# A row-modulated MLP and routed low-rank layer on one core: the last block's sixth and seventh outer products on two levels, its first rows leaving by accumulating stores

## The chip, the cores and the metric

The kernel runs on one core of a Trainium2 chip. The metric is device time in microseconds (us), the median of the runs shown. All arithmetic is in float32.

## The reference, cut to what matters

```python
# cond: x (64, 64, 512), q (64, 256)
q_emb = relu(q @ W3 + b3)
v = (n * x + sum(x, axis=1, keepdims=True)) * q_emb[:, None, :]
y = relu(v @ W2 + b2)                       # first 512x512 product
# ffn
base = y @ W_base + b_base                  # second 512x512 product
shared = (y @ A_s) @ B_s                    # rank 16
gates = softmax(y @ W_router + b_router)    # 6 experts
w = gates where among the two largest, else 0
routed = sum_e w_e * (y @ A_r[e]) @ B_r[e]  # rank 16 each
out = x + base + shared + routed
```

There are 4096 rows of 512 features.

## The kernel before, in words

The rows lie transposed, features on the 128 partitions. They are worked in four blocks (`k` = 0 to 3) of 1024 rows; a block has two halves `h` of 512 rows and two pairs `f` of 128-feature chunks.

Each 512x512 product is done by a Strassen scheme (the form with seven products and shared sums): over the two row halves and two feature halves, seven outer products, numbered 1 to 7, replace eight. `row_sums` makes the sums of rows (`sy`), `weight_sums` those of weights (`tb`, `t2`). An outer product can itself be done by the same scheme, in seven 128x256 products instead of eight: this is "two levels". `inner_row_steps` makes its four row sums, `inner_weight_side` its four weight sums.

An outer product on two levels is called by its place `t` in a list `order`. Its inner products are the calls `q(n, t)`, n = 1 to 7, into two PSUM banks, `a` and `b`, each split in a low half `lo` and a high half `hi`: 1 and 2 go to a-lo, 5 and 3 to a-hi, 6 to b-lo, 7 and 4 to b-hi. The chain between them is:

- `seed_y(t)`: ScalarE copies a-lo to b-lo; q(6, t) adds on top of it.
- `seed_z(t)`: ScalarE copies b-lo to b-hi; q(7, t) adds on top, and `take_22(t)` reads b-hi out before q(4, t) adds again.
- `take_w5(t)`, `take_u(t)`, `take_22(t)`, `take_11(t)`, `take_12(t)` and `take_21(t)` bring the results out to SBUF. They are copies on ScalarE where nothing is added (`plus` is None), and additions on VectorE else; `take_1` is `take_11` and `take_12`.

In the second product of block 3 (`second_inner`), `order` is (1, 2, 5, 4, 3): these five are on two levels. Outer products 6 and 7 are plain: `product(bank["y", j], 6, ...)` and `product(bank["z", j], 7, ...)`, four 128x512 matmuls each, seeded by `seed` on ScalarE. Their results are added to `x12`, `x21` and `x22`, the tiles of the residual rows, by VectorE. `x11` takes p1 (on GpSimd), the second outer product and the routed part (`pr`, on VectorE), and leaves by `leave` on SyncE's queue.

The instructions of each engine run in the order in which the Python code issues them; waits are on semaphores. `gate` makes the softmax and the ranks from `ph` on VectorE, with other work placed in it by `between`; `weigh` makes `hw`, `turn` transposes it to `hwT` (TensorE, then two ScalarE copies), `routed` adds the low-rank part to a bank. `difference` makes `hwd` on GpSimd. GpSimd also makes most inner row sums and issues the accumulating stores (`accum_op=ALU.add`) of blocks 1 and 2, whose rows had been written from `x1` to the output in DRAM beforehand, in `load_rows`.

`first_inner` is the first product of blocks 1 to 3, on two levels throughout; `relus` writes y; POOL's L603 and L606 make `e3` and the last `p5`. `wide_sums` lays out the weight sums of the second product's inner levels.

Of the kernel before, what the change touches and what calls it, by code (L numbers as in the profile page):

```python
# [16 lines left out]
P = 128  # L17
# [21 lines left out]
def adaln_ffn(ctx: ExitStack, tc: tile.TileContext, xa, x0, x1, head, w3, w2, wb, a, bcat, bb, br, outT):  # L39
# [117 lines left out]
    def inner_weights(w, t, groups):  # L157

        low = w.rearrange("p (o k) m -> p o k m", k=KH)
        place, steps = {}, []  # L160
        for it, outer, engine in groups:
            if outer == (1, 2):
                b = lambda c, m: low[:, :, c, ts(m, P)]
            elif outer == (3,):
                b = lambda c, m: t[3][:, c, ts(m, P)].unsqueeze(1)
            else:
                step = 3 // (len(outer) - 1)
                b = lambda c, m, step=step: t["sums"][:, ::step, c, ts(m, P)]
            place.update((o, (it, n)) for n, o in enumerate(outer))
            steps.append(inner_weight_side(it, b, engine))  # L170

        def side(o, n):
            b = {1: t[o][:, 0, :P], 2: t[o][:, 1, :P], 3: t[o][:, 1, P:]}
            it, i = place[o]
            return b[n] if n in b else it[:, {5: 0, 6: 1, 7: 2, 4: 3}[n], i]

        return side, steps
# [302 lines left out]
    def first_inner(k, y):  # L480
# [98 lines left out]
        for step in inner[k]["late"]:  # L579
            step()  # L580
        fill(2)
        for t in range(2, 7):
            open_banks(t)
            take_1(t - 2)
            q(1, t)
            q(5, t)
            seed_y(t)
            q(4, t - 2)
            take_21(t - 2)
            q(7, t - 1)  # L590
            take_22(t - 1)
            if t > 2:
                take_u(t - 1)
            take_w5(t)
            fill(1)
            q(3, t - 1)
            q(6, t)
            seed_z(t)
            if t > 2:
                q(2, t - 1)  # L600
            if order[t - 2] == 6:
                for cols in (hi, lo):
                    nc.gpsimd.tensor_tensor(e3[:, :, cols], u[:, :, cols], p5[:, :, cols], ALU.add)  # L603
            if order[t - 2] == 7:
                for cols in (lo, hi):
                    nc.gpsimd.tensor_tensor(p5[:, :, cols], v7[:, :, cols], p5[:, :, cols], ALU.add)  # L606
            if order[t - 2] == 2:
                relus(p1, 0, 0)
            fill((1, 1, 2, 2, 0)[t - 2])
# [8 lines left out]
        relus(p5, KH, 1)  # L618
# [27 lines left out]
    def turn(k):  # L646
        pt = ps_h.tile([P, 2 * NS, P], F32, tag="ph", name=f"pt_{k}")
        hwT = small.tile([P, 2, TB], F32, tag="hwT", name=f"hwT_{k}")
        for s in range(2 * NS):
            nc.tensor.transpose(pt[:GB, s, :], hw[:, s, :], ident)  # L650
        for h in range(2):
            nc.scalar.copy(hwT[:GB, h], pt[:GB, ts(h, NS)].rearrange("p s t -> p (s t)"))  # L652
        return hwT
# [6 lines left out]
    def gate(k, ph, between=()):  # L660
# [30 lines left out]
        nc.vector.tensor_tensor(eq, gj, ge, ALU.is_equal)  # L691
        others()
        nc.vector.tensor_tensor(gt, gj, ge, ALU.is_gt)
        nc.vector.tensor_tensor(eq, eq, tri.unsqueeze(1).to_broadcast(pair), ALU.mult)
        nc.vector.tensor_tensor(gt, gt, eq, ALU.add)
# [5 lines left out]
    def load_rows(k):  # L701

        res = {}
        for n, (f, h) in zip(pair_tags[2:3] + pair_tags[:2] + pair_tags[3:], ((1, 0), (1, 1), (0, 0), (0, 1))):
            if (f, h) == (0, 0) and 0 < k < NB - 1:

                nc.sync.dma_start(outT[k, :KH, h], x1[k, :KH, :, ts(h, TB)])
                continue
# [6 lines left out]
    def second_between(k, y, res):  # L715
# [72 lines left out]
        def main_part(ph):  # L788
# [40 lines left out]
            hwT = turn(k)  # L829
# [45 lines left out]
    def second(k, y, ph, res):  # L875
# [65 lines left out]
        hwT = turn(k)  # L941
# [134 lines left out]
    def second_inner(k, y, res):  # L1076


        order = (1, 2, 5, 4, 3)
        lo, hi = slice(0, R2), slice(R2, TB)  # L1080
        plain = xpool.tile([P, NC, 2, TB], F32, tag="x", name="inner_y").rearrange("p c h t -> p (c h t)")
        plain = plain.rearrange("p (n o t) -> p n o t", n=4, o=4)
        parts = mid.tile([P, 4, KH, TB], F32, tag="s", name=f"parts_{k}")
        p1, p5 = (parts[:, n] for n in range(2))
        x11, x12, x21, x22 = res[0, 0], res[1, 0], res[0, 1], res[1, 1]
# [4 lines left out]
        s_side, sums_of = row_places(lambda o: sy[o], {o: (plain[:, :, i], at) for o, (i, at) in places.items()})  # L1090
        plus = {1: None, 2: x11, 5: None, 4: x21, 3: x12}
        out = {1: p1, 2: x11, 5: p5, 4: x21, 3: x12}

        def passed_on(t, j, cols):
            o = order[t]
            if o == 5:
                add(x12[:, j, cols], x12[:, j, cols], p5[:, j, cols])
                add(x22[:, j, cols], x22[:, j, cols], p5[:, j, cols], nc.gpsimd)
# [19 lines left out]
        of_y = lambda f, h: lambda c, r: y[:, f + c, h, ts(r, R2)]  # L1118
        run(sums_of(1, of_y(0, 0), nc.gpsimd))

        def row_side():
# [5 lines left out]
            fourth.extend(steps[3:])  # L1127

        def late_sums():
            of_s = lambda o: lambda c, r: sy[o][:, c, ts(r, R2)]  # L1130
            run(sums_of(5, of_s(5), nc.gpsimd))
            run(sums_of(4, of_y(KH, 1), nc.gpsimd))
            run(fourth)
            run(sums_of(3, of_s(3), nc.gpsimd))
# [3 lines left out]

        def first_part():
            open_banks(0)  # L1140
            q(1, 0)
            q(5, 0)
            seed_y(0)
            take_w5(0)
# [6 lines left out]
        def leave(f, h, t):  # L1151
            for j in range(KH):
                nc.sync.dma_start(outT[k, f + j, h], t[:, j])

        def seed(j, name, source):
            bank[name, j] = ps_p.tile([P, TB], F32, tag="pp", name=f"o{name}_{k}_{j}")
            nc.scalar.copy(bank[name, j], source)

        def main_part(ph):
            open_banks(1)  # L1160
            q(1, 1)
            q(5, 1)
            seed_y(1)
# [11 lines left out]
            gate(k, ph, (first, lambda: tools.take_12(0)))  # L1175
            q(4, 0)
            take_21(0)
            q(7, 1)
            take_22(1)
            take_u(1)  # L1180
            q(3, 1)
            q(2, 1)
            weigh(k, ph)
            late_sums()
            take_1(1)
            for j in range(KH):
                seed(j, "y", p1[:, j])
                product(bank["y", j], 6, j, tb, sy, start=False)
            q(4, 1)
            take_21(1)  # L1190
            for j in range(KH):
                seed(j, "z", bank["y", j])
                add(x12[:, j], bank["y", j], x12[:, j])
            product(bank["z", 0], 7, 0, tb, sy, start=False)
            hwT = turn(k)
            hws["second"] = hwT[:GB, 1]
            product(bank["z", 1], 7, 1, tb, sy, start=False)
            for j in range(KH):
                for x in (x21, x22):
                    add(x[:, j], bank["z", j], x[:, j])  # L1200
            add(x11, x11, p1, nc.gpsimd)
            hws["less"] = difference(k, hwT)[:GB]

            for t in (2, 3):
                open_banks(t)
                q(1, t)
                q(5, t)
                seed_y(t)
                take_w5(t)
            pr = ps_h.tile([P, 2 * NS, P], F32, tag="ph", name=f"pr_{k}")  # L1210
            pr = pr.rearrange("p (j s) t -> p j (s t)", j=KH)
            for j in range(KH):
                accumulate(pr[:, j], bcat_sb[:, ts(j, P)], hwT[:GB, 0], True)
            add(x11, pr, x11)
            leave(0, 0, x11)
            q(2, 2)
            q(6, 2)
            take_u(2)
            seed_z(2)
            q(3, 2)  # L1220
            routed(2, 1)
            q(6, 3)
            take_u(3)
            seed_z(3)
            q(7, 2)
            routed(2, 22)
            take_22(2)
            q(2, 3)
            take_1(2)
            open_banks(4)  # L1230
            q(1, 4)
            q(5, 4)
            seed_y(4)
            q(4, 2)
            routed(2, 4)
            take_21(2)
            q(7, 3)
            routed(3, 22)
            take_22(3)
            take_w5(4)  # L1240
            q(3, 3)
            q(6, 4)
# [4 lines left out]
                    for n, (b, at) in enumerate(((bank["b", 4], slice(R2, R2 + P)), (other, slice(0, P))))]  # L1247
            for n, b, cols in last:
                nc.scalar.copy(b, bank["b", 4][:, ts(n, P)])
            routed(3, 1)  # L1250
            take_1(3)
            q(4, 3)
            routed(3, 4)
            take_21(3)
# [5 lines left out]
            take_u(4)  # L1260
            q(3, 4)
            q(2, 4)
            routed(4, 1)
            take_1(4)
# [26 lines left out]
    def wide_sums():  # L1291
        place = xpool.tile([P, NC, 2, TB], F32, tag="x", name="inner_tb").rearrange("p c h t -> p (c h t)")
        wide["parts"] = place[:, 12 * P : 12 * P + 2 * KH * TB].rearrange("p (n j t) -> p n j t", n=2, j=KH)
        place = place[:, : 12 * P].rearrange("p (n o m) -> p n o m", n=4, o=3)
        high, wide["steps"] = inner_weights(
            wb_sb, tb, [(place[:, :, :2], (5, 4), nc.gpsimd), (place[:, :, 2:], (3,), nc.gpsimd)]
# [3 lines left out]
    for k in range(NB):  # L1300
        y = mid.tile([P, NC, 2, TB], F32, tag="y", name=f"y_{k}")
# [4 lines left out]
        else:  # L1306
# [4 lines left out]
            if k == 1:  # L1311
                for step in wide["steps"][1]:
                    step()
# [87 lines left out]
```

## Time and profile before

| | us |
|---|---|
| median of 3 runs | 253.21 (253.17 to 253.36) |
| span of the profiled execution, first to last instruction | 251.6 |
| TensorE busy | 246.9 |
| VectorE busy | 203.0 |
| ScalarE busy | 158.1 |
| GpSimd busy | 126.1 |
| granted TensorE clock | 1.000 |

No time of the profiled execution other than its span is recorded; the span lies 1.6 us below the median.

In the profile PE is TensorE, PEld its weight loads, DVE VectorE, ACT ScalarE, POOL GpSimd, SP SyncE. A row of a timeline gives start, duration, engine, line of the kernel, operation, what is written from what, shapes, and in brackets the idle time ahead of it and what ended it. TensorE does one float32 matmul in two passes, and each is a record: "x2" is one 128x256 product, "x4" two of them or one pair. Block 3 begins at about 189.7 us, its second product at about 216 us.

### The profile page before, as it was taken

The page shows a single profiled execution, that of the slowest core. Times are in us where ns is not written, and L with a number is a line of the kernel's source. Part 1 is how long each engine was busy: PE and PEld are TensorE (multiplying, and loading weights), DVE is VectorE, ACT ScalarE, POOL GpSimd, SP SyncE. Part 2 cuts the span into 40 slices and gives each one's busy share as a digit, 9 for nine tenths or more (in the row PEclk, how much of TensorE's full clock was granted, in tenths as well). Part 3 has the DMA queues.
Part 4 walks back from the last instruction along what each step waited for, and adds up shares of the span by engine and source line. Part 5 has one row for each costly group of instructions (what it writes and reads, how often), then busy time and mean ns, then how long its engine had stood idle before and what let it go on. Part 6 is the DMA issues. An engine that isn't in the chain of part 4 may idle for free.

```text
span 251.6 us, 3678 instructions
## 1 busy us (share of the span) xinstructions
PE 246.9 (98%) x1134; PEld 189.5 (75%) x1134; DVE 203.0 (81%) x407; ACT 158.1 (63%) x436; POOL 126.1 (50%) x150
## 2 busy tenths in 40 slices
PE   8999999999999999999999999999999999999993
PEld 4745897454468889857888889957888889966783
DVE  2899998879996888999994788999992577797472
ACT  2299588579017889797638889796836428252320
POOL 1000000009707589059479978339649984059850
PEclk9999999999999999999999999999999999999999
DMA  6998818000431024835559923306269953400054
GB/s 182 364 343 288 330 32 304 0 3 9 157 125 42 3 86 180 319 123 217 68 82 198 154 85 104 124 26 249 20 81 194 157 134 92 164 1 0 6 195 136
DMA packets 17482, 33.82 MB, mean 134 GB/s; under 512 B 1605, under 2 KB 3781, under 8 KB 17462
## 3 DMA queue, kind: packets, MB, share of 16 engines
q1 hardware_dynamic: 13910, 27.09, 30.6%
q0 software_dynamic: 3264, 6.29, 15.9%
q10 hardware_dynamic: 288, 0.20, 0.3%
q8 instruction: 9, 0.15, 0.2%
q14 instruction: 11, 0.09, 0.1%
HBM read 19.94 MB, written 14.68 MB: 138 GB/s over the span
## 4 chain that ended last, share of the span: by engine, by line
PE 98%; DVE 0%; issue 0%
PE ia L502 14%; PE ph L1338 11%; PE ib L502 11%; PE ha L988 10%; PE hb L988 8%; PE oz L181 7%; PE py L409 6%; PE oy L181 6%; PE ja L988 4%; PE jb L988 3%; PE ox L181 3%; PE ow L181 3%; PE idle L192 2%; PE yw L181 1%; PE pt L650 1%; PE yx L416 1%
## 5 line engine op out<-in xcount | busy, mean ns | idle before, releaser
L229 ACT ACTIVATE x<-x,vsum,nq 128x64 f32<-128x64 f32 x176 | 63.2, 432 | 1.0 <-DVE vsum L221 1.0
L657 POOL TENSOR_TENSOR hwd<-hwT 113x512 f32<-113x512 f32 x4 | 5.1, 1272 | 55.4 <-ACT hwT L652 55.4
L1338 PEld LDWEIGHTS ph<-a_sb,y 128*128 128x128 f32 x256 | 30.6, 192 | 0.7
L1338 PE MATMUL ph<-a_sb,y 128*128 128x118 f32 x256 | 30.6, 274 | 0.0
L493 DVE TENSOR_TENSOR u<-ib,u 128x256 f32<-128x256 f32 x42 | 16.4, 418 | 13.0 <-PE ib L502 12.9
L493 DVE TENSOR_TENSOR u<-ia,u 128x256 f32<-128x256 f32 (+1 forms) x36 | 16.0, 461 | 6.2 <-ACT u L540 4.7
L508 ACT COPY ib<-ia 128x256 f32<-128x256 f32 x21 | 7.6, 361 | 18.0 <-PE ia L502 18.0
L395 ACT ACTIVATE y<-u,head_sb 128x256 f32<-128x256 f32 (+1 forms) x30 | 15.8, 584 | 3.6 <-DVE u L468 3.0
L502 PE MATMUL ib<-inner_s,inner_t 128*128 128x256 f32 x60 | 17.4, 379 | 0.0
L219 DVE TENSOR_REDUCE vsum<-x 128x8 f32<-128x512 f32 x24 | 15.4, 674 | 0.0
L181 PE MATMUL oz<-sy,tb 128*128 128x512 f32 x32 | 15.0, 592 | 0.0
L181 PE MATMUL oy<-sy,tb 128*128 128x512 f32 x32 | 14.7, 598 | 0.0
L409 PE MATMUL py<-v,w_sb 128*128 128x512 f32 (+1 forms) x40 | 14.7, 518 | 0.0
L511 ACT COPY ib<-ib 128x256 f32<-128x256 f32 x21 | 7.6, 360 | 8.9 <-PE ib L502 8.5
L502 PEld LDWEIGHTS ib<-inner_s,inner_t 128*128 128x128 f32 x60 | 11.4, 190 | 1.6
L344 POOL TENSOR_TENSOR sy<-sy 128x256 f32<-128x256 f32 x4 | 3.8, 952 | 17.2 <-PE oy L181 17.2
L409 PEld LDWEIGHTS py<-v,w_sb 128*128 128x128 f32 x40 | 7.6, 196 | 6.2 <-issue 4.5
L267 ACT ACTIVATE v<-x,vsum,nq 128x64 f32<-128x64 f32 x32 | 11.1, 430 | 1.9 <-DVE vsum L265 1.9
L181 PEld LDWEIGHTS oy<-sy,tb 128*128 128x128 f32 x32 | 5.8, 190 | 6.8 <-issue 6.2
L745 POOL DMA_DIRECT2D out_dram<-y x8 | 10.7, 1723 | 0.0
L502 PE MATMUL ia<-s,t 128*128 128x256 f32 x36 | 10.2, 379 | 0.0
L181 PEld LDWEIGHTS oz<-sy,tb 128*128 128x128 f32 x32 | 5.8, 190 | 5.8 <-issue 5.3
(321 smaller groups left out, 679.4 us busy)
## 6 DMA issues: line engine op xcount, KB each, us to landing
xu<-in_x_dram SPq DMA_DIRECT2D x14, 512.0 KB, 4.6
out_dram<-xu SPq DMA_DIRECT2D x25, 256.0 KB, 2.1
x<-in_x_dram SPq DMA_DIRECT2D x12, 512.0 KB, 7.6
out_dram<-y POOLq DMA_DIRECT2D x8, 512.0 KB, 8.5
out_dram<-inner_tb POOLq DMA_DIRECT2D x4, 512.0 KB, 6.0
x<-in_x_dram SPq DMA_DIRECT2D x7, 256.0 KB, 5.9
w_sb<-in_w_dram SPq DMA_DIRECT2D x4, 256.0 KB, 5.7
wb_sb<-in_wb_dram SPq DMA_DIRECT2D x4, 256.0 KB, 5.1
```

What stands on the lines that cost most here:

```text
L181: nc.tensor.matmul(ps, w[i][:, c, ts(j, P)], s[i][:, c, :], start=start and c == 0, stop=c == KH - 1, skip_group_check=True,)
L219: nc.vector.tensor_reduce(vsum[:, c, bs], xc, AX.XY, ALU.add)
L229: nc.scalar.activation(x, x, AF.Identity, bias=bias, scale=scale)
L267: nc.scalar.activation(v[:, c, :, ts(b, NH)], batches_of(c, b, b + 1)[:, :, 0], AF.Identity, bias=vsum[:, c, b : b + 1], scale=nq[:, c, b ...
L395: nc.scalar.activation(y[:, f, h, cols], src, AF.Relu, bias=b2_sb[:, f : f + 1])
L409: nc.tensor.matmul(p[:, :, lo * NH : hi * NH], w2_sb[:, c, ts(f, P)], v[:, c, :, lo * NH : hi * NH], start=(c == 0 and lo == 0), stop=(c = ...
L493: add = lambda o, a, b: nc.vector.tensor_tensor(o, a, b, ALU.add)
L502: nc.tensor.matmul(bank[b, t][:, cols], t_side(o, n), s_side(o, n), start=n == 1, stop=True, skip_group_check=True,)
L508: nc.scalar.copy(bank["b", t][:, lo], bank["a", t][:, lo])
L745: nc.gpsimd.dma_start(outT[k, f : f + KH, h].rearrange("f p t -> p f t"), parts[o], accum_op=ALU.add)
L988: nc.tensor.matmul(p, w, s, start=start, stop=True, skip_group_check=True)
L1338: nc.tensor.matmul(ph[:, h * NS + s, :HC], y[:, c, h, ts(s, P)], a_sb[:, c, :], start=(c == 0), stop=(c == NC - 1),)
```

## The change

It touches seven things.

1. `order` becomes (1, 2, 6, 7, 5, 4, 3): the outer products 6 and 7 of block 3 are on two levels, at t = 2 and 3; products 5, 4 and 3 move to t = 4, 5 and 6. The steps of all seven are interleaved anew. Product 6 gives `u` = p1 + it, product 7 gives `z` = u + it, both kept in SBUF and added to x12, x21 and x22 as whole 128x1024 tiles.
2. Their row sums are eight new GpSimd operations beside the gate, their weight sums four 128x128 GpSimd operations in block 1 (sixth) and four in block 3 (seventh). The row sums of product 4 move ahead of those of product 1.
3. `x11` is gone. Block 3's first rows are copied from DRAM to DRAM, as in blocks 1 and 2, and p1, p2 and the routed part `r11` are added by three accumulating stores from GpSimd's queue. `r11` is copied out of PSUM by ScalarE.
4. The DRAM-to-DRAM copies are written with the 128 partitions as their first dimension.
5. The gate's ranks are made in three operations in place of four, in all four blocks.
6. In block 3 `hwd` is made by VectorE, from `hwT` and from `pt` in PSUM; the relus of p5 move ahead, between seed_y(6) and q(4, 4) of the first product.
7. `y` of block 3 is placed in a buffer of x, and its inner sums in that of y.

```diff
-            elif outer == (3,):
-                b = lambda c, m: t[3][:, c, ts(m, P)].unsqueeze(1)
+            elif len(outer) == 1:
+                b = lambda c, m, o=outer[0]: t[o][:, c, ts(m, P)].unsqueeze(1)
...
-        for step in inner[k]["late"]:
+        for step in inner[k]["late"] + (wide["steps"][2] if k == 1 else []):
             step()
...
             seed_y(t)
+            if t == 6 and k == NB - 1:
+                relus(p5, KH, 1)
             q(4, t - 2)
...
-        nc.vector.tensor_tensor(eq, gj, ge, ALU.is_equal)
+        nc.vector.tensor_tensor(gt, gj, ge, ALU.subtract)
         others()
-        nc.vector.tensor_tensor(gt, gj, ge, ALU.is_gt)
-        nc.vector.tensor_tensor(eq, eq, tri.unsqueeze(1).to_broadcast(pair), ALU.mult)
-        nc.vector.tensor_tensor(gt, gt, eq, ALU.add)
+        nc.vector.scalar_tensor_tensor(eq, gt, 0.0, tri.unsqueeze(1).to_broadcast(pair), ALU.is_equal, ALU.mult)
+        nc.vector.scalar_tensor_tensor(gt, gt, 0.0, eq, ALU.is_gt, ALU.add)
         others()
...
-        order = (1, 2, 5, 4, 3)
+        order = (1, 2, 6, 7, 5, 4, 3)
...
-        plus = {1: None, 2: x11, 5: None, 4: x21, 3: x12}
-        out = {1: p1, 2: x11, 5: p5, 4: x21, 3: x12}
+        plus = {1: None, 2: None, 6: p1, 7: u, 5: None, 4: x21, 3: x12}
+        out = {1: p1, 2: p2, 6: u, 7: z, 5: p5, 4: x21, 3: x12}
...
+        run(sums_of(4, of_y(KH, 1), nc.gpsimd))
         run(sums_of(1, of_y(0, 0), nc.gpsimd))
+
+        def to_rows(t, f=0, h=0):
+            nc.gpsimd.dma_start(
+                outT[k, f : f + KH, h].rearrange("f p t -> p f t"), t, accum_op=ALU.add
+            )
...
+            for o in (6, 7):
+                run(sums_of(o, of_s(o), nc.gpsimd))
 
         def late_sums():
+            to_rows(p1)
             run(sums_of(5, of_s(5), nc.gpsimd))
-            run(sums_of(4, of_y(KH, 1), nc.gpsimd))
             run(fourth)
+            to_rows(p2)
             run(sums_of(3, of_s(3), nc.gpsimd))
```

The new order of block 3's second product, from the gate on (what it replaces is told above):

```python
def second():
    tools.take_12(0); q(4, 0); take_21(0)
    start(2)                      # q(1, 2), q(5, 2), seed_y(2)
    q(7, 1); take_u(1); q(3, 1); take_22(1)

def third():
    q(2, 1); take_1(1); q(6, 2); seed_z(2); q(2, 2); take_w5(2)
    q(4, 1); take_21(1); q(7, 2); take_u(2); start(3)

gate(k, ph, (first, second, third))
weigh(k, ph)
late_sums()
q(3, 2); q(6, 3); seed_z(3); q(2, 3); start(4); q(7, 3)
take_22(2); take_w5(3); q(4, 2); take_1(2); take_21(2); take_w5(4)
q(3, 3); take_u(3); take_22(3)
hwT, pt = turn(k)
q(6, 4); take_u(4); seed_z(4); q(4, 3); take_1(3); take_21(3)
nc.vector.tensor_tensor(hwd[:GB], hwT[:GB, 0], of_h(1), ALU.subtract)
start(5); add(x21, x21, z); take_w5(5); q(2, 4); q(3, 4); routed(4, 1)
...                               # pr: two 113x512 matmuls
add(x22, x22, z)
r11 = ...                         # two ScalarE copies of pr
to_rows(r11)
take_1(4); q(6, 5); take_u(5); seed_z(5); q(7, 4); routed(4, 22); take_22(4)
q(2, 5); add(x12, x12, u); start(6)
q(4, 4); routed(4, 4); take_21(4); q(7, 5); routed(5, 22); take_22(5)
add(x12, x12, p5); take_w5(6); q(3, 5); q(6, 6)
...                               # the tail, as before
```

## The prediction

> **What bounds the kernel now.** I read the page's busy table and its chain first, then TensorE's timeline in the last block, then the other engines' timelines in the same stretch.
>
> ```profile
> PE 246.9 (98%) x1134; PEld 189.5 (75%) x1134; DVE 203.0 (81%) x407; ACT 158.1 (63%) x436; POOL 126.1 (50%) x150
> ...
> PE 98%; DVE 0%; issue 0%
> ```
>
> TensorE (PE) is busy for 246.9 of 251.6 us and the chain that ended last is PE alone: what shortens PE's own list shortens the kernel, and every new wait of PE lengthens it one for one. PE's timeline around the work that goes:
>
> ```profile
> 222.93 0.59 PE L988 MATMUL ja<-y,wb_sb 128*128 128x256 f32 x2
> 223.36 3.65 PE L181 MATMUL oy<-sy,tb 128*128 128x512 f32 x8
> 226.85 0.59 PE L988 MATMUL jb<-y,low_t 128*128 128x256 f32 x2
> 227.28 1.88 PE L181 MATMUL oz<-sy,tb 128*128 128x512 f32 x4
> 229.00 1.04 PE L650 MATMUL pt<-ident,hw 128*113 128x128 f32 x8
> 229.88 1.88 PE L181 MATMUL oz<-sy,tb 128*128 128x512 f32 x4
> 231.59 0.59 PE L988 MATMUL ja<-sy,tb 128*128 128x256 f32 x2
> ```
>
> Columns: start, duration, what. Durations overlap; the distance between starts is the price. No bracket of idle time stands in any row: PE has no gap here. I call one q(n,t), a 128x256 product, a step; ten of them fill 219.04 to 223.36, 0.432 us each.
>
> **TensorE's list.** The plain sixth and seventh products go: 3.49 (223.36 to 226.85), 1.72 and 1.71 us, 6.92 in all. Fourteen steps come: 14 x 0.432 = 6.05. Net -0.87. The two products for hwT (pr) and the tail stay. Without new waits: 253.21 - 0.87 = 252.34. The profiled span is 251.6, 1.6 below the median of the runs; I take those 1.6 us as unchanged, and put the difference on the median.
>
> **What a late copy costs PE.** Each two-level product needs the y-bank copied (seed_y) between its q(5,t) and q(6,t), and q(7,t)'s result taken before q(4,t) adds on top of it. The price of such a wait:
>
> ```profile
> 216.40 0.59 PE L988 MATMUL ja<-inner_y,low_t 128*128 128x256 f32 x2
> ...
> 217.03 0.36 ACT L996 COPY jb<-ja 128x256 f32<-128x256 f32 x1 [2.79 <-PE ja L988]
> ...
> 222.67 1.11 ACT L1157 COPY oy<-parts 128x512 f32<-128x512 f32 x2
> ...
> 223.31 0.30 PEld L181 LDWEIGHTS oy<-sy,tb 128*128 128x128 f32 x2 [0.19 <-ACT oy L1157]
> ```
>
> The seed starts 0.63 us after q(5,0) and ends 0.99 after it. The oy copy (0.57 as a single one) ended near 223.25, 0.11 before PE's start at 223.36; the weight load came 0.05 later, and the 8 passes took 3.49 where 8 x 0.432 is 3.46. So a result that ends 0.11 ahead of its step costs about 0.03: the wait is (end minus planned start) + 0.14.
>
> *First new wait.* In the new order the seventh product (t = 3) goes q(1,3), q(5,3), q(3,2), q(6,3): q(6,3) is two steps, 0.86 us, behind q(5,3), but the seed ends 0.99 behind it. In the kernel before the tightest pair has three steps (219.48 to 220.77). Wait: 0.99 - 0.86 + 0.14 = 0.27. Not less than 0.13 (the bare difference), and a wait cannot gain; not over 0.35.
>
> *Second new wait.* q(4,4) must wait for take_22(4) on VectorE (DVE). DVE runs take_12(4), take_u(5), take_22(4) in this order, and take_12(4) waits for ScalarE's (ACT's) take_11(4), which the new code queues behind the two 128x512 copies of pr into r11. Counted from pr's first start: ACT can start at 1.92 (a pr pair lasts 1.88 in the timeline, plus 0.04), the two copies advance ACT by about 0.5 each (the hwT pair took 1.08), take_11 ends near 3.28, the three DVE operations (0.42 each, 0.34 apart) at 3.31, 3.65 and 3.99, the last ending at 4.41. PE reaches q(4,4) after pr (1.72) and six steps (2.59): 4.31. Wait: 4.41 - 4.31 + 0.14 = 0.24; take 0.25, bounds 0.10 and 0.35. In the kernel before DVE itself added pr to x11, and ACT's copies were not behind it.
>
> **VectorE in the gate.** The three rank operations replace four: L691, L693, L694 and L695 are 0.46, 0.45, 0.45 and 0.46 (0.87 in block 3). A scalar_tensor_tensor of 128x256 is 0.42 (L255), so 288 elements are about 0.46: DVE saves one operation per block. PE is full in the gates of blocks 0 to 2, so that is worth nothing there. In block 3 the last DVE link matters: take_22(2) stands behind the gate and hw, and q(4,2) waits for it. Worked forward from unchanged rows: q(7,1) at 222.93, its bank read by ACT 223.56 to 223.93, take_22(1) to 224.37, two rank operations to 225.26, three takes of which the last waits for q(7,2) (225.52 + 0.63 = 226.15) and ends 226.57, rank 0.45, w 0.21, hw 1.08 to 228.37, take_22(2) to 228.70. It is due 0.14 before q(4,2): 229.41 + 0.27 - 0.14 = 229.54. Cover: 0.84.
>
> What can eat the cover is GpSimd (POOL). It was idle here for 10.36 us; now the eight row sums of the sixth and seventh products (0.73 each) run beside the gate, and the four of product 5 after them.
>
> ```profile
> 222.96 0.45 DVE L694 TENSOR_TENSOR eq<-eq,tri 128x288 f32<-128x288 f32 x1
> 223.44 0.87 DVE L695 TENSOR_TENSOR gt<-gt,eq 128x288 f32<-128x288 f32 x1
> ...
> 224.83 0.21 DVE L699 SCALAR_TENSOR_TENSOR w<-rank,g 128x48 f32<-128x48 f32 x1
> ...
> 223.18 0.81 POOL L344 TENSOR_TENSOR inner_y<-sy 128x256 f32<-128x256 f32 x1 [10.36 <-PE ja L988]
> ```
>
> L695 lost 0.41 when a POOL sum had just started; L699 lost nothing with POOL still at work. Three such operations (two rank ones and w) follow take_22(1). At 0.2 each, the mean of these two rows, they lose 0.6, of which 0.31 is DVE's wait for q(7,2) anyway: covered. At a full POOL sum each, 2.2 - 0.31 = 1.9, less the cover: 1.05 us of stall. I take 0.05. The operations ahead of take_22(1) have 1.3 us of waiting to lose. The Trainium skill (SBUF — State Buffer, "Who interferes with whom") says that a DVE instruction with both inputs in SBUF and a GpSimd instruction that reads SBUF exclude each other for a whole instruction, whoever comes second waiting fully; it speaks against this change, since by it all three could wait out a full sum, which is the 1.05, while the two rows give 0.05.
>
> **Covered elsewhere.** POOL's four 128x128 weight operations (0.46) in block 1 fit the 2.08 us it idled ahead of L603; if not, e3 is late one for one. The four in block 3 end near 208.7. The relus of p5, moved ahead of seed_z(6), start when L606 ends (206.99), take 1.33, and seed_z(6) ends at 208.67; q(7,6) at 208.88 needs it by 208.74: 0.07 of cover, beyond it one for one. SP has one load less into SBUF and a copy from DRAM to DRAM instead, due only when p1 leaves at 223 or later. DVE loses six adds of 0.64 and the 1.23 pr add, gains twelve takes of 0.42, the 1.22 adds and hwd (0.69, due before pr, done near 233.5 against 234.8): off the path but for the links above. Placing y in x's buffers and inner_y in y's waits for the previous block's stores, issued at 197.84 at the latest, first needed near 208.7.
>
> *The accumulating stores.* POOL is in order, and each store waits for the one before to land:
>
> ```profile
> 179.25 1.19 POOL L745 DMA_DIRECT2D out_dram<-inner_tb  x1
> 185.84 1.20 POOL L745 DMA_DIRECT2D out_dram<-inner_tb  x1 [5.39 <-DVE inner_s L344]
> ```
>
> One alone: 6.6 us from issue to the next. Behind p1 (223 to 225) are queued the sums of 5, the fourth row sum and p2 (by 232), behind p2 the sums of 3 (first needed at 238.7), behind r11 (by 238.6) the x22 adds, 3.5 us, and on SP every x22, x21 and x12 store. r11 lands near 245, the last stores go at about 247.5: covered, with 3 us.
>
> **Sum.** -0.87 + 0.27 + 0.25 + 0.05 = -0.30: 252.91, own range 252.6 to 253.2.
>
> **Rivals.** *PE absorbs the two waits* (252.34 to 252.7): the wait rule rests on one row, and a step of copy may be shorter than the rows I used. For it: no gap anywhere in the last block before. Against it: two steps are 0.86 and the copy needs 0.99. It gives over 0.51 us if both waits together stay under 0.35. *GpSimd's sums hold up the gate* (slower): at take_22(2), price up to 1.05, giving 252.91 + 1.00 = 253.91; slower than before once DVE is over 1.2 us late on that link, slower by 0.51 from 1.7 on. L695 speaks for it, L699 against. *The stores' chain ends last* (slower): if both landings take the longest the trace has (11.6, three in flight together), p2 goes at 235, r11 at 247, the x22 adds end at 251 and the span is about 4 us longer, 257; decided near 9 us a landing. Against it: nothing else is on the DMA engines there (DMA share 0.00 from 219 to 232). That the fourteen steps bring no saving is excluded by the rows.
>
> **Chances.** Forecast 0.42, absorbed 0.36, gate 0.13, stores 0.06, other waits 0.03. 0.2%, 0.51 us, is about what a measurement of this kernel can tell from no change. Faster 0.36, within 0.42, slower 0.22. Range 252.35 (no wait at all) to 253.8 (nearly all of the gate's bound).
>
> **What would show it.** Right: PE busy about 0.87 less; a weight load of q(6,3) (jb) released by ACT's seed and one of q(4,4) released by DVE, 0.2 to 0.3 us of lost PE start each. Wrong: even steps of 0.432 at both places (absorbed); a gap at q(4,2) with rank operations of 0.8 or more (gate); POOL's r11 store after 242 and SP's stores bunched behind it (chain).

## The result, and the profile after

| | before | after |
|---|---|---|
| median, us | 253.19 (6 runs, 253.01 to 253.53) | 254.62 (6 runs, 254.22 to 255.19) |
| ratio, 95% interval | | 1.006 [1.0046, 1.0074] |
| span of the profiled execution | 251.6 | 252.8 |
| from the start of TensorE's 201st matmul record to that of its last | 200.34 | 201.98 |
| from there to the end of SyncE's last instruction, 0.05 ahead of the span's end | 4.00 | 4.09 |
| granted TensorE clock | 1.000 | 0.997 |

The change is slower by 1.43 us; 252.91 was forecast, with a range to 253.8. The fourth row is the one to compare: up to the 201st matmul record the same work takes a few tenths more or less in each execution (47.19 us before, 46.72 after). From there on the kernel lost 1.63 us (taken before the two figures are rounded).

Busy line and chain of the page after:

```profile
PE 246.9 (98%) x1146; PEld 191.3 (76%) x1146; DVE 208.3 (82%) x407; ACT 159.7 (63%) x442; POOL 135.3 (53%) x167
...
PE 89%; POOL 4%; DVE 4%; issue 1%; ACT 1%; POOLq 0%; ACTq 0%
```

PE's busy time is no smaller although its list is shorter: of the waits below only 1.15 us, the two brackets in the rows that follow, show as idle time; the rest counts as busy. The chain is no longer PE alone; VectorE and GpSimd have come into it. TensorE's waits show as distances between starts above 0.432 for a step. Its timeline after, in two stretches of the last block:

```profile
226.21 0.59 PE L993 MATMUL ja<-outer_y,seventh_tb 128*128 128x256 f32 x2
227.50 0.70 PE L993 MATMUL ja<-outer_y,tb 128*128 128x256 f32 x2 [0.69 <-DVE parts L986]
228.03 0.59 PE L993 MATMUL jb<-outer_y,seventh_tb 128*128 128x256 f32 x2
...
242.84 1.03 PE L993 MATMUL ja<-hwT,bcat_sb 113*128 113x256 f32 x4
244.32 0.70 PE L993 MATMUL jb<-y,inner_tb 128*128 128x256 f32 x2 [0.46 <-DVE xu L986]
```

q(3, 2) starts 1.29 us behind q(5, 3), not 0.43, and the step after it 0.53 behind it: 0.96 lost. q(4, 5) starts 1.48 behind a row of two steps (0.86): 0.62, with the next step 0.72. Summed over all places of the trace, from the starts of the records:

| wait of TensorE | us |
|---|---|
| q(7, 6) of the first product, behind ScalarE's seed_z(6) | 0.27 |
| q(3, 2), behind VectorE's take_w5(2) | 0.96 |
| q(4, 2), q(3, 3), behind hw and take_22(2) | 0.32 |
| q(4, 4), behind VectorE's take_22(4) | 0.23 |
| q(4, 5), behind VectorE's take_22(5) | 0.72 |

Together 2.50; less the 0.87 of the list that is +1.63, which is the 1.63 found. What held VectorE at the two large ones, from the timelines of VectorE and of GpSimd:

```profile
224.13 0.74 DVE L696 SCALAR_TENSOR_TENSOR eq<-gt,tri 128x288 f32<-128x288 f32 x1
224.91 1.87 DVE L697 SCALAR_TENSOR_TENSOR gt<-gt,eq 128x288 f32<-128x288 f32 x1
226.70 0.41 DVE L986 TENSOR_TENSOR outer_y<-ja,outer_y 128x256 f32<-128x256 f32 x1
...
240.00 3.93 DVE L986 TENSOR_TENSOR xu<-xu,parts 128x1024 f32<-128x1024 f32 x1
```

```profile
223.84 0.72 POOL L347 TENSOR_TENSOR outer_y<-sy,outer_y 128x256 f32<-128x256 f32 x1
224.50 1.19 POOL L1132 DMA_DIRECT2D out_dram<-parts  x1
225.28 1.17 POOL L344 TENSOR_TENSOR inner_y<-sy 128x256 f32<-128x256 f32 x1
226.53 0.83 POOL L345 TENSOR_TENSOR inner_y<-inner_y,sy 128x256 f32<-128x256 f32 x1
...
239.77 3.07 POOL L986 TENSOR_TENSOR xu<-xu,parts 128x512 f32<-128x512 f32 x3
```

The last rank operation (L697) took 1.87 us instead of the 0.46 of its kind: it ended 0.33 after GpSimd's sum L344 (226.45). take_w5(2) stands behind it on VectorE. The addition x12 += u took 3.93 instead of 1.22: it ended 1.09 after the third of GpSimd's additions to x22 (242.84). take_22(5) stands behind that. In both, the time from the end of that GpSimd operation to VectorE's own end is what VectorE's operation takes alone less 0.13 (0.46 and 1.22 alone), as if its work began about when GpSimd was through. The take at 226.70, with one of its two inputs in PSUM, took its usual 0.41 beside GpSimd's sum L345.

### The profile page after: what moved, and what is told of

Its sections match the earlier page's. It is cut to its first block, busy times and chain, and to the rows that moved or that the text cites. A ratio compares the mean times of both kernels' runs of the same rounds, so it can differ in the third digit from the quotient of the medians.

```text
span 252.8 us, 3725 instructions
## 1 busy us (share of the span) xinstructions
PE 246.9 (98%) x1146; PEld 191.3 (76%) x1146; DVE 208.3 (82%) x407; ACT 159.7 (63%) x442; POOL 135.3 (53%) x167
## 4 chain that ended last, share of the span: by engine, by line
PE 89%; POOL 4%; DVE 4%; issue 1%; ACT 1%; POOLq 0%; ACTq 0%
PE ia L502 12%; PE ph L1372 11%; PE ha L993 10%; PE ib L502 9%; PE hb L993 8%; PE py L409 6%; PE oz L181 5%; PE oy L181 4%; PE ja L993 4%; PE ox L181 3%; PE ow L181 3%; PE jb L993 2%; DVE xu L986 2%; PE idle L192 1%; PE yw L181 1%; PE pt L653 1%
## 5 line engine op out<-in xcount | busy, mean ns | idle before, releaser
L660 POOL TENSOR_TENSOR hwd<-hwT 113x512 f32<-113x512 f32 x3 | 3.8, 1266 | 54.9 <-ACT hwT L655 54.9
L344 POOL TENSOR_TENSOR sy<-sy 128x256 f32<-128x256 f32 x4 | 3.8, 946 | 18.3 <-PE oy L181 18.3
L181 PE MATMUL oz<-sy,tb 128*128 128x512 f32 x24 | 11.3, 592 | 0.0
L181 PE MATMUL oy<-sy,tb 128*128 128x512 f32 x24 | 11.1, 597 | 0.0
L750 POOL DMA_DIRECT2D out_dram<-inner_tb x4 | 4.9, 1232 | 10.1 <-ACT y L1009 10.1
L245 DVE TENSOR_REDUCE vsum<-x 128x8 f32<-128x512 f32 (+1 forms) x10 | 5.7, 574 | 4.4 <-DMA x<-in_xa_dram 3.5
```

The lines of the kernel that those rows point to most:

```text
L181: nc.tensor.matmul(ps, w[i][:, c, ts(j, P)], s[i][:, c, :], start=start and c == 0, stop=c == KH - 1, skip_group_check=True,)
L750: nc.gpsimd.dma_start(outT[k, f : f + KH, h].rearrange("f p t -> p f t"), parts[o], accum_op=ALU.add)
```

## The experiments

All start from the kernel after, unless said otherwise. "Before" is the kernel before on the same chip in the same comparison. Waits are read as above.

| run | median | ratio to before, 95% interval |
|---|---|---|
| e1 | 253.85 | 1.0044 [1.0027, 1.0061] |
| e2 | 255.93 | 1.0128 [1.0108, 1.0147] |
| e3 | 254.43 | 1.007 [1.0041, 1.01] |
| e4 | 254.23 | 1.0048 [1.0036, 1.006] |
| e5 | 255.49 | 1.0096 [1.0081, 1.0111] |
| e6 | 253.42 | 1.002 [1.0003, 1.0038] |
| e7 | 255.58 | 1.0109 [1.0082, 1.0136] |
| e8 | 252.86 | 0.9986 [0.9971, 1.0] |
| e9 | 254.12 | 1.0051 [1.003, 1.0073] |
| e10 | 253.69 | 1.0029 [1.0019, 1.004] |
| e11 | 253.84 | 1.0047 [1.0022, 1.0071] |
| e12 | 252.95 | 0.9999 [0.9983, 1.0015] |
| e13 | 259.34 (one run) | |
| e14 | 253.82 | 1.0006 [0.9985, 1.0027] |
| e15 | 252.53 | 0.998 [0.997, 0.9989] |

### e1: the addition x12 += u earlier

```diff
             add(x22, x22, z)
+            add(x12, x12, u)
...
             q(2, 5)
-            add(x12, x12, u)
```

> One addition on VectorE moves: x12 += u (128x1024) goes from its place ahead of take_22(5) to the one behind x22 += z, where GpSimd is idle and VectorE itself idled 1.83 us. Theory (VectorE's additions from SBUF are held while GpSimd adds from SBUF): it takes 1.2 instead of 3.93 us, take_22(5) starts about 1.5 us earlier, the wait of TensorE at q(4, 5) (0.73) goes: 254.6 - 0.7 = 253.9. Rival (q(4, 5) stands behind something else, such as the stores' traffic or ScalarE's copies): 254.6.

253.85. The wait at q(4, 5) is gone, the other waits in the last block are as before the edit (0.90 at q(3, 2), 0.32, 0.23). The two additions, x22 += z and x12 += u, now take 1.18 us each:

```profile
235.39 2.36 DVE L986 TENSOR_TENSOR xu<-xu,parts 128x1024 f32<-128x1024 f32 x2
```

The term is shown: 0.7 us in the trace, by where this one addition stood (in the medians, 0.81 above before instead of 1.43).

### e2 and e3: GpSimd's stores in another order

```diff
# e2
-            to_rows(p1)
             run(sums_of(5, of_s(5), nc.gpsimd))
             run(fourth)
+            to_rows(p1)
             to_rows(p2)
```

> GpSimd's accumulating store of p1 moves behind the four row sums of product 5 and the fourth row sum, so the sums of 7 and of 5 follow one another without a store between. Theory A (each GpSimd sum from SBUF holds VectorE's two-input operations, the store adds nothing): the second rank operation stays held, 0.9 to 1.9 us, and the time stays 254.6 within 0.3. Theory B (issuing the store holds VectorE, too): the second rank operation falls to 0.9 or less, the wait at q(3, 2) from 0.96 to 0.3 or less, and the time to 253.9 to 254.0. Both theories leave the wait at q(4, 5) as it is.

```diff
# e3
-            to_rows(p1)
+            to_rows(p2)
             run(sums_of(5, of_s(5), nc.gpsimd))
             run(fourth)
-            to_rows(p2)
+            to_rows(p1)
```

> The stores of p1 and p2 change places. p2 is complete later, so GpSimd waits from the end of product 7's sums (224.6) to about 226, and VectorE's second rank operation (224.9) finds it idle; no work is left out. Theory (GpSimd's work beside it holds the rank operation, sum or store): 0.46 instead of 1.87 us, no wait at q(3, 2); the wait of 0.27 that I had forecast at q(6, 3) comes out instead; q(4, 2) and q(3, 3) lose theirs of 0.2: 254.6 - 0.96 + 0.27 - 0.2 = 253.7. Rival (the three-operation form or ScalarE is what is slow): 254.6.

The rank operation and what GpSimd did beside it, in e2's and then in e3's timelines:

```profile
224.66 0.86 DVE L697 SCALAR_TENSOR_TENSOR gt<-gt,eq 128x288 f32<-128x288 f32 x1
```

```profile
224.26 0.94 POOL L344 TENSOR_TENSOR inner_y<-sy 128x256 f32<-128x256 f32 x1
```

```profile
225.11 0.46 DVE L697 SCALAR_TENSOR_TENSOR gt<-gt,eq 128x288 f32<-128x288 f32 x1
```

```profile
226.46 1.20 POOL L1132 DMA_DIRECT2D out_dram<-outer_y  x1 [1.69 <-ACT outer_y L1009]
```

With sums following one another it waits for one sum (it ends 0.32 after it); with GpSimd idle (e3, where p2's store waits until 226.46) for none. In both the waits at q(3, 2), q(4, 2) and q(3, 3) are gone and q(6, 3) shows 0.40. In e2, TensorE from q(5, 3) on, and the seed:

```profile
225.95 0.59 PE L993 MATMUL ja<-outer_y,seventh_tb 128*128 128x256 f32 x2
226.38 0.59 PE L993 MATMUL ja<-outer_y,tb 128*128 128x256 f32 x2
227.14 0.67 PE L993 MATMUL jb<-outer_y,seventh_tb 128*128 128x256 f32 x2 [0.16 <-ACT jb L1001]
227.65 1.03 PE L993 MATMUL ja<-sy,tb 128*128 128x256 f32 x4
```

```profile
226.64 0.36 ACT L1001 COPY jb<-ja 128x256 f32<-128x256 f32 x1 [0.98 <-PE ja L993]
```

That the hold is shorter and the wait at q(3, 2) gone is what I had expected of theory B in e2 (wrongly read, as e13 shows: not the store's issue, but the sum behind it) and of the theory in e3. Neither time follows, as other links break. In e2 p2's store waits for p1's landing until 236.00, r11's goes at 242.44, and the end comes 6.99 us behind the last matmul instead of 4.09. In e3 r11's store moves to 240.50, GpSimd's x22 additions with it, and now x12 += p5 stands beside them: 3.52 us, and 1.32 of wait at q(3, 6).

### e4: the takes ahead of the rank operations

```diff
         nc.vector.tensor_tensor(gt, gj, ge, ALU.subtract)
         others()
+        if k == NB - 1:
+            others()
```

> In block 3 the third group of work inside the gate (take_12(1), take_w5(2), take_u(2) and what goes with them) is put ahead of the last two rank operations instead of behind them. Theory (q(3, 2) stands behind the held rank operations through take_w5(2)): the wait at q(3, 2) goes (-0.96), q(6, 3) shows its 0.27, hw is not later than now, a wait of up to 0.3 at q(4, 2) stays: 253.8 to 254.0. Rival (take_w5(2) itself would be held as long, since it comes late for another reason): 254.6.

254.23. No wait at q(3, 2), 0.40 at q(6, 3), 0.48 at q(4, 2) and q(3, 3), 0.72 at q(4, 5). So q(3, 2) did wait for the takes behind the held rank operation; the wait behind hw is 0.18 more than I allowed.

### e5, e6 and e7: five places mended, and two of them taken back

```diff
# e5: e3's order of the stores, and
-                q(7, 2)
                 take_u(2)
                 start(3)
+                q(7, 2)
...
             add(x22, x22, z)
+            add(x12, x12, u)
+            take_1(4)
...                                   # the copies into r11
-            to_rows(r11)
-            take_1(4)
...
-            add(x12, x12, u)
...
             take_21(4)
+            to_rows(r11)
...
-            if t == 6 and k == NB - 1:    # first product
-                relus(p5, KH, 1)
...
-        if k < NB - 1:
-            relus(p5, KH, 1)
+        relus(p5, KH, 1)
```

> Five places mended together, no work left out: p2's store ahead of p1's; x12 += u behind x22 += z; take_1(4) ahead of the copies into r11 and r11's store behind the three x22 additions of GpSimd; q(7, 2) behind start(3); the relus of p5 in block 3 back at their old place. Theory (each wait of TensorE in the last block has its own holder, and all are removed): no wait is left, the net of the lists, -0.87, shows: 253.1 - 0.9 = 252.2, up to 252.6 if one small wait comes back; VectorE's x12 += p5, next to GpSimd's additions to x22 in the run before this, may be held up to 1 us and is covered. Rival (waits only move: something else of the fuller GpSimd and VectorE becomes late): 253.5 or more.

e6 is e5 with the relus of p5 early:

> As the run with all five mended, but the relus of p5 stay ahead of seed_z(6), as in the change. Theory (their cover of 0.07 is a toss of how long GpSimd's last p5 addition takes): 0 to 0.3 later than the other, a wait of 0 to 0.3 at q(7, 6), by execution. Rival (their early place is worth something, as y is ready earlier): 0.2 or more earlier than the other.

e7 is e5 with q(7, 2) ahead of start(3):

> As the run with all five mended, but q(7, 2) ahead of start(3), as in the change, so that q(6, 3) is only two steps behind q(5, 3). Theory (the copy of seed_y(3) is a step short): a wait of 0.2 to 0.27 at q(6, 3), the time later by as much. Rival (TensorE absorbs it): the same time within 0.1.

e5 was 3.3 us slower than I expected, and e6 2.1 faster than e5: the rival on the relus held, far above its 0.2. GpSimd's timeline of e5 at the first row sum of the second product:

```profile
212.23 0.73 POOL L344 TENSOR_TENSOR inner_y<-y 128x256 f32<-128x256 f32 x1 [3.80 <-ACT y L395]
```

In the change this sum starts at 208.56. The change put product 4's sums ahead of product 1's, and they read the part of y that the relus of p5 write: with late relus the first of the eight sums starts 3.7 us later and the last 5.9, they run beside VectorE's row sums (up to 0.94 instead of 0.41 each), and TensorE waits 0.69 at q(5, 0), 0.34 at q(6, 0) and 0.71 a little later. The early relus are not an ornament: they pay for the order of the sums. In e6 only 0.22 is left at q(7, 2) and 0.1 at q(4, 4), and TensorE's stretch is 199.79, 0.55 below before. But r11's store, now issued at 241.38, is in flight with the last rows, whose last two landings take 2.9 and 2.7 us instead of 2.2 and 1.9, and the end is 4.84 behind the last matmul.

e7 against e5 gives the seed's price: 0.40 at q(6, 3), in place of 0.73 at q(7, 2), which e5's own edit had brought (its take_u(2) is issued ahead of q(7, 2) and writes out the same bank). The two medians, 0.09 apart, are what the rival said, but for another reason: the wait was not absorbed, one wait took the place of another, and 0.35 at q(4, 4) came with it.

### e8: two parts of the change alone

The kernel before with the three rank operations and the new form of the DRAM copies.

> The kernel before with two parts of the change alone: the ranks in three operations, in all four blocks, and the copies from DRAM to DRAM written with the partitions first. Theory (both lie beside a full TensorE): the time of the kernel before within 0.2. Rival (they carry part of the loss, or of the gain): 0.3 or more from it, in either direction.

252.86, 0.9986 [0.9971, 1.0]: no loss comes from these two; a gain of up to 0.7 us is not excluded. The median lies 0.37 below before, more than the 0.2 that I allowed; but from the 201st matmul record on, where three of the four gates lie, the profile shows 200.36 us against 200.34, so it shows no gain there.

### e9, e10 and e11: r11's store early again

```diff
# e9: e3's order of the stores, relus early, and
+                start(3)
                 q(7, 2)
                 take_u(2)
-                start(3)
...
             add(x22, x22, z)
+            add(x12, x12, u)
+            tools.take_11(4)
...                                   # r11 and its store
-            take_1(4)
+            tools.take_12(4)
+            passed_on(4, slice(0, KH), lo)
...
-            add(x12, x12, u)
# e10: e9 with p1's store first
# e11: e9, and
-   add(x22[:, j, cols], x22[:, j, cols], p5[:, j, cols], nc.gpsimd)
+   add(x22[:, j, cols], x22[:, j, cols], p5[:, j, cols], nc.gpsimd if cols == hi else nc.vector)
...
-            passed_on(4, slice(0, KH), lo)
...
             take_22(4)
+            passed_on(4, slice(0, KH), lo)
```

> The change with four places mended, the relus of p5 left early: p2's store ahead of p1's; x12 += u behind x22 += z; take_11(4) ahead of the copies into r11, r11's store still ahead of GpSimd's x22 additions; q(7, 2) behind start(3), and take_u(2) behind q(7, 2). Against the run with r11's store at the end (0.22 us of wait at q(7, 2), and an end 4.84 instead of 4.0 to 4.1 us behind the last matmul): the wait at q(7, 2) goes, the end is 4.1 again, x12 += p5 is held by the x22 additions and take_w5(6) comes 0 to 0.3 late: 253.1 - 0.87 + 0.1 + 0.2 = 252.5. Rival (waits only move): 253.3 or more.

> As the mended kernel, but with p1's store first again, so that GpSimd issues it and goes on to product 5's sums while VectorE does the second rank operation. Theory (that hold alone costs what it cost in the change): the second rank operation 1.8 to 1.9 us, q(3, 2) late by 0.9 and q(4, 2) and q(3, 3) by 0.3 in all: 1.0 to 1.3 us above the mended kernel. Rival (with the other waits gone it is covered): less than 0.4 above it.

> As the mended kernel, but the first of the three x22 additions (128x512) is made by VectorE, in the 2.2 us in which it waits for q(7, 5), not by GpSimd. Theory (GpSimd's additions hold x12 += p5): GpSimd is through about 1 us earlier, x12 += p5 falls to 1.3 us or so, and a wait at q(3, 6), if the mended kernel has one, goes: 0 to 0.3 below the mended kernel, 252.3 to 252.5. Rival (VectorE is what is full there): 0.2 or more above it.

e9 missed by 1.6 us, and the rival held: the waits moved. take_u(2) behind q(7, 2) makes hw 1.2 us later than in e6, counted from q(5, 3) (0.77 at q(4, 2) and q(3, 3)); GpSimd's sums of product 3, later by p2's store and the fourth row sum, now hold VectorE's additions, so that take_12(4) is late (0.66 at q(4, 4)); x12 += p5 took 2.59 (0.39 at q(3, 6)). In e10 the hold of the rank operation is back (1.86 us, 0.87 at q(3, 2), 0.32), yet it is 0.43 faster than e9, because its sums of 3 are early and q(4, 4) and q(3, 6) do not wait. So p1's store first was not wrong by itself; each order had its own collision. In e11 x12 += p5 took 1.22 and q(3, 6) did not wait; its median is 0.28 below e9's, inside their spread.

### e12, e14 and e15: an order without a wait

```diff
# e12: e11, and
-                start(3)
-                q(7, 2)
                 take_u(2)
+                start(3)
...
             q(3, 2)
+            q(7, 2)
             q(6, 3)
# e15: e12, and
-            add(x12, x12, u)         # behind x22 += z
...
             passed_on(4, slice(0, KH), lo)
+            add(x12, x12, u)
# e14: e15, and the relus of p5 behind seed_z(6)
```

> The change with p2's store ahead of p1's, x12 += u behind x22 += z, take_11(4) ahead of the copies into r11 with r11's store next on GpSimd, the first x22 addition on VectorE, and q(7, 2) moved behind q(3, 2) with take_u(2) left ahead of it: q(6, 3) is then three steps behind q(5, 3), and take_u(2) is not behind q(7, 2). Theory (a wait is gone when its holder ends earlier, and hw is as early as in the run without a wait at q(4, 2)): waits of 0.1 to 0.3 in all, an end 4.1 behind the last matmul: 253.0 - 0.87 + 0.2 + 0.1 = 252.4. Rival (VectorE and GpSimd are too full for any order; a wait of 0.6 or more comes at another place): 253.2 or more.

> As the run before with q(7, 2) behind q(3, 2), which had two waits left (0.21 at q(7, 6), 0.32 at q(4, 4)), with two more places changed: x12 += u goes behind take_22(4) and the x22 addition on VectorE, where VectorE waited 1.33 us for q(7, 5), so that take_12(4) and take_22(4) stand behind one addition held by GpSimd's sums of product 3 less; and the relus of p5 go behind seed_z(6) instead of ahead of it. Theory (each wait has its own holder): both waits go, -0.87 + 0.1 of a later end is left: 253.1 - 0.8 = 252.3, faster than both kernels. Rival (VectorE and GpSimd are too full for any order): a wait of 0.4 or more at q(4, 5) or q(3, 6), or in the sums of product 4: 252.9 or more.

> As the run before, but the relus of p5 ahead of seed_z(6) again, as in the change. In the run before, TensorE lost 1.16 us where the router's first matmuls waited for the relus, and nothing behind that. Theory (each wait has its own holder, and the relus' place costs 0 to 0.3 here and more at either other place): the wait of the router's matmuls goes, 0 to 0.3 at q(7, 6) stays, all others are gone: 253.2 - 0.87 + 0.15 + 0.15 = 252.6, faster than both kernels by 0.4 or more. Rival (too full in any order): 253.0 or more.

e12 came out level with before: 0.36 left at q(4, 4), where x12 += u still stood beside a sum of product 3, and 0.21 at q(7, 6). e14, 1.5 above what I expected, had no wait behind the gate, but 1.16 where the router's first matmuls waited for the late relus. e15 has no wait of the last block at all: from the 201st matmul record to the last 199.45 us, 0.89 below before; the end is 4.09 behind it. 252.53 against 253.05, ratio 0.998 [0.997, 0.9989]: faster than before, by 0.52 in the medians, and so faster than both kernels. VectorE's timeline of e15 at the two places that had cost most:

```profile
224.80 0.46 DVE L697 SCALAR_TENSOR_TENSOR gt<-gt,eq 128x288 f32<-128x288 f32 x1
...
237.94 1.91 DVE L986 TENSOR_TENSOR xu<-xu,parts 128x512 f32<-128x512 f32 x2
```

The second row is the x22 addition and x12 += u, 1.91 us together, in the gap in which VectorE waits for q(7, 5).

### e13: the store alone beside the rank operation

```diff
             to_rows(p1)
+            to_rows(p2)
             run(sums_of(5, of_s(5), nc.gpsimd))
             run(fourth)
-            to_rows(p2)
```

> The order of the change, but p2's store directly behind p1's on GpSimd: behind p1's store GpSimd then waits some 6 us for its landing, and the second rank operation stands beside the issue of a store alone, with no sum after it. Only its duration is read; the time is 2 to 4 us longer, as product 5's sums come late. Theory S (the issue of a store holds it as a sum does): 1.0 us or more. Theory T (only sums hold; in the change it lost its turn to the sum that followed the store): 0.46 to 0.7.

VectorE's and GpSimd's timelines:

```profile
224.63 0.46 DVE L697 SCALAR_TENSOR_TENSOR gt<-gt,eq 128x288 f32<-128x288 f32 x1
```

```profile
224.22 1.18 POOL L1132 DMA_DIRECT2D out_dram<-parts  x1
230.57 1.20 POOL L1132 DMA_DIRECT2D out_dram<-outer_y  x1 [5.17 <-DMA out_dram<-parts]
```

The rank operation starts 0.41 us into the issue of the store, as in the change, and takes 0.46. Theory T holds: the issue of a store did not hold this operation; what held it for 1.87 us in the change was the sum queued directly behind the store, 0.33 after whose end it ended.

## Why the prediction was wrong, point by point

- **TensorE's list, -0.87: right.** e15's profile, with no wait left, measured -0.89. Its median gained 0.52 (interval 0.28 to 0.76); what the executions that were not profiled lost of the rest, nothing here shows.
- **First new wait, q(6, 3): mechanism right, mis-sized.** 0.40 in e2, e3, e4 and e7, above its upper bound of 0.35. The seed ended 1.05 us behind q(5, 3) in e2 (226.64 + 0.36 against 225.95), not 0.99, and a step after a wait stands 0.51 ahead of the next, which the rule (end + 0.14) left out. In the change itself it was hidden behind the larger wait at q(3, 2).
- **Second new wait, q(4, 4): right.** 0.25 forecast, 0.23 measured (starts at 239.58, 240.14 and 240.68), behind the take that was named.
- **"What can eat the cover is GpSimd", 0.05: the step that failed.** It cost 1.28. First, the links were not all listed: I priced only take_22(2), behind hw, but take_w5(2) stands behind the same rank operations, and q(3, 2) has less cover (0.66 by the rows of the forecast, an estimate). Second, the price was a mean of two rows of before (0.2) where the operation waits for whole operations of GpSimd: 1.41 here. e3 and e13 (0.46) against e1 and e10 (1.86) show it. The three operations together lost 2.11 (0.28, 1.41 and 0.42), which is nearly the 2.2 of my own bound. Third, the two rows were misread. L695 ended 0.32 after the end of GpSimd's sum (223.99): it waited out what was left of the sum. L699, my row against it, started only 0.07 before the end of the next sum, so it had next to nothing to lose:

```profile
224.07 0.83 POOL L345 TENSOR_TENSOR inner_y<-inner_y,sy 128x256 f32<-128x256 f32 x1
```

The Trainium skill's rule, which I set beside the rows (SBUF — State Buffer, "Who interferes with whom"), was nearer than my mean of them; read in this way, the rows agree with it.
- **VectorE's additions "off the path but for the links above": the second failure.** x12 += u, costed at 1.22 and covered, took 3.93 beside GpSimd's x22 additions and cost 0.72 at q(4, 5) (e1). The same collision was to be priced here too.
- **The relus' cover of 0.07: too thin.** 0.27 in the change's profile, 0.13 to 0.21 in e3 and e12, 1.41 in e11's profiled execution, none in e1, e2, e4, e6, e9, e10 and e15: it hangs on when GpSimd's last p5 addition ends (in e11 the relus waited 1.62 us for it). That the sums of product 4 need them early (e5) I had not seen.
- **Stores covered with 3 us: right for the change** (the end moved by 0.09), but not for every order (e2, e6).
- **Ranks, copies, weight sums at nothing: right** (e8 for the first two; for the weight sums, TensorE shows no new wait in block 1 of the profile after, and those in block 3 end at 208.60, where 208.7 was forecast).

The rival "GpSimd's sums hold up the gate" had the mechanism, at 253.91; it lacked q(3, 2) and the second place, x12 += u.

## What to carry to other kernels

When work is added to GpSimd, list every VectorE operation with two inputs in SBUF that will run beside it and everything that stands behind each on VectorE, and give each a cover of whole GpSimd operations, not a mean slowdown. A new order has as many links as it has takes: mending one wait shifts both engines, and the next collision may cost as much (e3, e5, e9), so judge an order by all its waits. The same list of matmuls gave 252.53 us in e15 and 255.49 in e5.

## What the runs showed of the hardware that was not expected

- A VectorE operation can be held for longer than one GpSimd operation: x12 += u ran 3.93 us through three additions of GpSimd in a row (3.07 in all), where in e2 the rank operation got its turn after one sum. Which of the two happens, these runs do not settle.
- The issue of an accumulating store does not hold VectorE's two-input operation (0.46 beside it, e13). The Trainium skill (SBUF — State Buffer, "Who interferes with whom") infers that tensor_tensor takes only the read interface of the port pair that VectorE shares with GpSimd, and that making a DMA's descriptors needs its write interface; the row agrees with that, for a scalar_tensor_tensor. Why the operation, 0.37 us on its way when the sum behind the store starts in the records, was still held to that sum's end (1.86 to 1.87 in three kernels) stays open.
- The hold goes both ways: in e15, beside VectorE's 128x1024 additions, a GpSimd sum of 0.73 took 1.60 us, and one directly behind a store's issue, 1.15 to 1.21 where no such addition runs beside it, took 1.75.
